# A four-layer graph network on one core: seven products of 384 columns in layer 3, the last two groups kept side by side, due times set anew

## The chip, the core and the metric

The kernel runs on one core of a Trainium2 chip. The core has TensorE (PE, matrix products, whose weight loads stand in the profile as PEld), VectorE (DVE), ScalarE (ACT), GpSimd (POOL) and DMA queues. The metric is the device time of one execution in microseconds; times given for the kernel are medians of several runs. Everything is computed in float32.

## The reference

There are 128 graphs of 64 nodes with 256 features. Four layers follow each other, each of the form "normalize over the features, take the positive part, apply the layer, add the result to x":

```
h = max(layernorm(x), 0);  x = x + layer_i(h)

layers 0, 1: masked attention, 8 heads of 32 features, softmax over the 64 nodes of a graph
layer 2:     five times: m = h @ weight[l]; agg = A^T m
             gi = agg @ w_ih^T + b_ih;  gh = h @ w_hh^T + b_hh
             r, z = sigmoid(i_r + h_r), sigmoid(i_z + h_z);  n = tanh(i_n + r * h_n)
             h = (1 - z) * n + z * h
layer 3:     norm = (sum |adj| + 1e-6) ** -0.5
             f = (h @ theta) * norm;  f_hom = (adj @ f) * norm
             f_het = h @ W_h;  gate = sigmoid(h @ W_t + b_t)
             elu(gate * f_hom + (1 - gate) * f_het)
```

The change concerns the three products of layer 3 (theta, W_t, W_h, each 256 by 256) and the order in which the work of all layers is issued.

## The kernel before

**Tiling.** Two graphs make a pair of 128 tokens, four pairs a group of 512 tokens, and a half is two pairs. There are 16 groups. Nothing is exchanged between groups, so the work of several stands side by side.

**Stages of a group.** `front` (line 909) does the attention of layers 0 and 1, one half after the other (`attend`, line 496), and prepares what the adjacency gives: A, norm and the transposed adjacency adjT. `entry` (957) normalizes x into h, transposed, for layer 2. `gru` (702) is a generator: each `next` adds one of the five steps of layer 2. `back` (966) takes the two halves of layer 3 through `back_half` (971): h is transposed back (hx, 978) and added to x, x is normalized into hT (through L452 and L457), and then each pair has its products: f (998), two matmuls of 256 columns, and gate (1004), two of 512, with W_t and W_h beside each other in w_th. DVE scales f by norm (1001), adds b_t (1007), ACT takes the tanh (1009) and copies het (1010). The product with adjT is hom (1011). Elementwise work follows to the store (1029).

**Layer 2 as it is already.** The GRU's products are taken as seven block products in place of eight (Winograd's form of Strassen's scheme): a product of two 2 x 2 block matrices needs seven block products if sums and differences of blocks are formed first. `combine` (648) forms those of the weights on GpSimd, once; `pre` (707) on GpSimd and `less` (795) on DVE form those of the data. The products accumulate in PSUM banks, which ACT copies out (`saved`, 806) and DVE adds (`summed`, 812) between products. In the profile all these matmuls stand at line 744. The weights of layer 2 are multiplied with w_ih before (`fuse_weights`, 662; products at 681), kept in DRAM, and loaded again for each step (`gv`).

**What sets the order.** Each operation is recorded in a `Plan` with an engine, an estimated cost, and what it reads and writes. `Plan.strand(base, span)` gives the recorded operations keys from base to base + span, along their TensorE work; a key is a due time in units of a group. `Plan.run` (165) first moves keys back so that an operation is due before what needs it, then plays the engines forward: it takes, over all engines, the operation that can start first, and among those that can start at about the same time the one of smallest key, as long as its key lies within AHEAD of the earliest open one. The order so found is written out, and each engine works through its own part in order. An operation that needs a buffer which isn't free can't be taken; the buffers are `Slots`, and those of the tags g, ht, agg, Ta, Th, gv, qT, kexp and v are given out in the order in which they were recorded. PSUM has four banks of tag "a" (attention, transposes, agg, layer 3) and four of tag "g" (the GRU's gates and the fusion of weights).

**Due times before (lines 1035 to 1062).** The first fronts have -1 to 0. The fusion of step l has -1 + 0.15 l, span 0.15. Front g + 1 has g, span 0.8; entry g - 0.1; step l of group g has g + 0.4 l - 0.2, span 0.4; back g + 2.2, span 0.9.

Of the kernel before, what the change touches and what calls it, by code (L numbers as in the profile page):

```python
# [10 lines left out]
AF = mybir.ActivationFunctionType  # L11
# [33 lines left out]


SWITCH, BESIDE, ALONE = 200, 0.3, 0.1
AHEAD = 1.2


def mm(n, count=1):
# [183 lines left out]
def gnn_stack_kernel(ctx: ExitStack, tc: tile.TileContext, a: dict, out: bass.AP):  # L235
# [18 lines left out]
    def new(tag, shape, n, name=None):  # L254
        if tag not in tags:
            home = psum if tag in ("a", "g") else dram if tag == "gates" else work
            tags[tag] = Slots(home, tag, n, tag in ("g", "ht", "agg", "Ta", "Th", "gv", "qT", "kexp", "v"))
        return Val(tags[tag], name or tag, shape)
# [17 lines left out]
    def sca(cost, fn, reads, writes, early=0.0):  # L276
        plan.add("ACT", cost, fn, reads, writes, early=early)
# [4 lines left out]
    def dma(kb, fn, reads, writes, n=1):  # L282
        plan.add("SP", max(450 * n, 60 + kb * 5), fn, reads, writes)
# [37 lines left out]
    def load_w(name, cols):  # L321
        t = new(f"w_{name}", [P, 2, cols], 1)
        dma(cols, lambda: nc.sync.dma_start(t.tile, a[name].rearrange("(c p) o -> p c o", p=P)), [], [t])
        return t
# [88 lines left out]
    with plan.strand(-0.3, 0.1):  # L413

        b_rz = new("b_rz", [P, 4], 1)
        vec(160, lambda: nc.vector.tensor_add(b_rz.tile, cols[:, 4:8], cols[:, 10:14]), [cols], [b_rz])
        vec(160, lambda: nc.vector.tensor_scalar(b_rz.tile, b_rz.tile, 0.5, None, op0=ALU.mult),
            [b_rz], [b_rz])


        b_n = new("b_n", [P, 2], 1)
        vec(160, lambda: nc.vector.tensor_sub(b_n.tile, cols[:, 8:10], cols[:, 14:16]), [cols], [b_n])

        theta = load_w("L3_gnn_theta", D)
        w_th = new("w_th", [P, 2, 2 * D], 1)
        for i, name in enumerate(("L3_gnn_W_t", "L3_gnn_W_h")):
            dma(256, lambda i=i, name=name: nc.sync.dma_start(
                w_th[:, :, i * D : (i + 1) * D], a[name].rearrange("(c p) o -> p c o", p=P)),
                [], [(w_th, i)])
        b_t = load_row("L3_gnn_b_t")  # L430
        blk = filled("adjblk", [P, PAIRS, P], 0.0)

# [212 lines left out]
        pe(470, weigh, reads, po, holds=[oT], small=True)  # L645
        finish()

    def combine(part, at):

        def one(dst, x, y, op):  # L650
            pool(1050, lambda: nc.gpsimd.tensor_tensor(at(dst), at(x), at(y), op=op), [part], [part])

        one(4, 1, 3, ALU.add)
        one(5, 4, 0, ALU.subtract)
        one(6, 2, 5, ALU.subtract)
        one(1, 0, 1, ALU.subtract)

# [2 lines left out]
    def fuse_weights(l):  # L662
# [7 lines left out]
                    nc.tensor.transpose(ps[:, ec * D + kc * P : ec * D + (kc + 1) * P],  # L670
                                        gw[l][:, kc, ec * P : (ec + 1) * P], ident.tile)

        wT = new("cp", [P, 2, D], 4, f"wT_{l}")
        pe(437, turn, [gw[l], ident], [ps], holds=[wT, gv])
        sca(act(512), lambda ps=ps, wT=wT: nc.scalar.activation(
            wT.tile, ps.tile.rearrange("p (c e) -> p c e", c=2), AF.Copy), [ps], [wT])
# [25 lines left out]
    def gru(h, ht, A, name):  # L702
# [19 lines left out]
        for l in range(LAYERS):  # L722
# [81 lines left out]
            less(3, lambda lo=lo: lo(1), lambda Ta=Ta: Ta[:, 1, :], [agg, (Ta, 1)])  # L804

            def saved(bk, n):
                t = new("cp", [P, 2, HALF], 4, f"{n}_{nm}")
                sca(act(512), lambda: nc.scalar.activation(
                    t.tile, bk.tile.rearrange("p (g t) -> p g t", g=2), AF.Copy), [bk], [t])
                return t  # L810
# [98 lines left out]
    def front(g):  # L909
# [38 lines left out]
        def turn():  # L948
# [1 line left out]
                nc.tensor.transpose(ps[:, p * P : (p + 1) * P], blk[:, p, :], ident.tile)  # L950

        pe(437, turn, [blk, ident], [ps], holds=[adjT])
        sca(act(512), lambda: nc.scalar.activation(
            adjT.tile, ps.tile.rearrange("p (t n) -> p t n", t=PAIRS), AF.Copy), [ps], [adjT])
        held[g] = xt, A, adjT, norm

    def entry(g, xt):

        h = new("h", [P, 2, TOK], 3, f"h_{g}")
        ht = new("ht", [P, PAIRS, D], 2, f"ht0_{g}")  # L960
        for half in range(2):
            norm_relu_t(xt, half, h, lambda half=half: h[:, :, half * HALF : (half + 1) * HALF],
                        [(h, (0, half)), (h, (1, half))], f"{g}_2_{half}", ht)
        return h, ht

    def back(g, xt, h, adjT, norm):

        for half in (1, 0):
            back_half(g, xt, h, adjT, norm, half)

    def back_half(g, xt, h, adjT, norm, half):
        ps = bank(f"hx_{g}_{half}")
# [9 lines left out]
        for i in range(2):  # L982
# [3 lines left out]
                xt[:, p, :], ps[:, i * D : (i + 1) * D], cols[:, 18 + t : 19 + t], xt[:, p, :],  # L986
                op0=ALU.mult, op1=ALU.add), [ps, cols, (xt, p)], [(xt, p)])
        hT = normed(xt, half, f"{g}_3_{half}")
        for p in range(2 * half, 2 * half + 2):
            nm = f"{g}_{p}"  # L990
            s = slice((p % 2) * P, (p % 2 + 1) * P)
            f = new("f", [P, D], 1, f"f_{nm}")
            gt = new("gt", [P, D], 2, f"gt_{nm}")
            het = new("het", [P, D], 2, f"het_{nm}")
            o = new("o", [P, D], 2, f"o3_{nm}")
            pf, pg, ph = bank(f"f_{nm}"), bank(f"gate_{nm}"), bank(f"hom_{nm}")
            for kc in range(2):
                pe(mm(256), lambda kc=kc, s=s, pf=pf: nc.tensor.matmul(  # L998
                    pf[:, :D], hT[:, kc, s], theta[:, kc, :], start=kc == 0, stop=kc == 1),
                    [hT, theta], [pf], holds=[f])  # L1000
            vec(dve(256, 1), lambda p=p, f=f, pf=pf: nc.vector.tensor_scalar(
                f.tile, pf[:, :D], norm[:, p : p + 1], None, op0=ALU.mult), [pf, norm], [f])
            for kc in range(2):
                pe(mm(512), lambda kc=kc, s=s, pg=pg: nc.tensor.matmul(  # L1004
                    pg.tile, hT[:, kc, s], w_th[:, kc, :], start=kc == 0, stop=kc == 1),
                    [hT, w_th], [pg], holds=[gt, het])
            vec(dve(256), lambda gt=gt, pg=pg: nc.vector.tensor_tensor(gt.tile, pg[:, :D], b_t.tile, op=ALU.add),
                [pg, b_t], [gt])
            sca(act(256, 0.3), lambda gt=gt: nc.scalar.activation(gt.tile, gt.tile, AF.Tanh, scale=0.5), [gt], [gt])
            sca(act(256), lambda het=het, pg=pg: nc.scalar.activation(het.tile, pg[:, D:], AF.Copy), [pg], [het])  # L1010
            pe(mm(256), lambda p=p, f=f, ph=ph: nc.tensor.matmul(
                ph[:, :D], adjT[:, p, :], f.tile, start=True, stop=True), [adjT, f], [ph], holds=[o])

            vec(dve(256, 1), lambda p=p, o=o, ph=ph, het=het: nc.vector.scalar_tensor_tensor(
                o.tile, ph[:, :D], norm[:, p : p + 1], het.tile, op0=ALU.mult, op1=ALU.subtract),
                [ph, norm, het], [o])
            vec2(dve(256), lambda o=o, gt=gt: nc.vector.scalar_tensor_tensor(
                o.tile, gt.tile, 1.0, o.tile, op0=ALU.add, op1=ALU.mult), [gt, o], [o])
            vec2(dve(256), lambda o=o, het=het: nc.vector.scalar_tensor_tensor(
                o.tile, o.tile, 0.5, het.tile, op0=ALU.mult, op1=ALU.add), [o, het], [o])  # L1020

            vec2(210, lambda o=o, gt=gt: nc.vector.tensor_scalar(gt.tile, o.tile, 0.0, None, op0=ALU.min),
                [o], [gt])
            sca(act(256, 0.3), lambda gt=gt: nc.scalar.activation(gt.tile, gt.tile, AF.Exp), [gt], [gt])
            vec2(dve(256), lambda o=o, gt=gt: nc.vector.scalar_tensor_tensor(
                o.tile, o.tile, 0.0, gt.tile, op0=ALU.max, op1=ALU.add), [o, gt], [o])
            vec2(dve(256), lambda p=p, o=o: nc.vector.scalar_tensor_tensor(
                xt[:, p, :], o.tile, -1.0, xt[:, p, :], op0=ALU.add, op1=ALU.add), [o, (xt, p)], [(xt, p)])
        dma(256, lambda: nc.sync.dma_start(
# [4 lines left out]

    held, chains = {}, {}
    parts = {g: front(g) for g in range(n_groups)}
    with plan.strand(-1.0):
        for g in (0, 0, 1, 0, 1, 0):
            next(parts[g])
        for _ in parts[0]:  # L1040
            pass
    for l in range(LAYERS):
        with plan.strand(-1.0 + 0.15 * l, 0.15):
            fuse_weights(l)
    with plan.strand(-0.2, 0.1):
        combine(w_hh, lambda b: w_hh[:, :, b, :])
    for at, g, l in sorted((g + 0.4 * l, g, l) for g in range(n_groups) for l in range(LAYERS)):
        if l == 0:
            xt, A, adjT, norm = held[g]
            with plan.strand(g - 0.1, 0.1):  # L1050
                h, ht = entry(g, xt)
            held[g] = xt, h, adjT, norm
            chains[g] = gru(h, ht, A, str(g))
            if g + 1 < n_groups:
                with plan.strand(g, 0.8):
                    for _ in parts[g + 1]:
                        pass
        with plan.strand(at - 0.2, 0.4):
            next(chains[g])
        if l + 1 == LAYERS:  # L1060
            with plan.strand(g + 2.2, 0.9):
                back(g, *held.pop(g))
    plan.run()

# [32 lines left out]
```

## Time and profile before

| what | value |
|---|---|
| median of 3 runs | 2589.91 us (2588.77 to 2590.13) |
| span of the profiled run | 2587.4 us |
| busy: PE, PEld | 2550.2, 2149.8 us |
| busy: DVE, ACT, POOL | 1863.6, 1357.7, 844.8 us |
| matmuls at line 744 (GRU), passes of 256 columns | 6720 |
| gate at line 1004, passes of 512 columns | 256 |
| f at line 998, passes of 256 columns | 256 |
| f scaled, L1001 | 64 times, 479 ns |
| gate + b_t, L1007 | 64 times, 419 ns |
| het copied, L1010 | 64 times, 383 ns |

A float32 matmul of the code stands in the trace as two passes with a weight load each. A pass's own duration overlaps its neighbours' (a pass of 256 columns is shown with 380 ns), so passes are best counted from start to start. "Idle before" is the time that an engine waited, with the operation that released it.

### The profile page before, as it was taken

The page shows a single profiled execution, that of the slowest core. Times are in us where ns is not written, and L with a number is a line of the kernel's source. Part 1 is how long each engine was busy: PE and PEld are TensorE (multiplying, and loading weights), DVE is VectorE, ACT ScalarE, POOL GpSimd, SP SyncE. Part 2 cuts the span into 40 slices and gives each one's busy share as a digit, 9 for nine tenths or more (in the row PEclk, how much of TensorE's full clock was granted, in tenths as well). Part 3 has the DMA queues.
Part 4 walks back from the last instruction along what each step waited for, and adds up shares of the span by engine and source line. Part 5 has one row for each costly group of instructions (what it writes and reads, how often), then busy time and mean ns, then how long its engine had stood idle before and what let it go on. Part 6 is the DMA issues. An engine that isn't in the chain of part 4 may idle for free.

```text
span 2587.4 us, 54651 instructions
## 1 busy us (share of the span) xinstructions
PE 2550.2 (99%) x22505; PEld 2149.8 (83%) x22505; DVE 1863.6 (72%) x3986; ACT 1357.7 (52%) x2536; POOL 844.8 (33%) x881
## 2 busy tenths in 40 slices
PE   8999999999999999999999999999999999999997
PEld 6788888888888888888888888888888888888875
DVE  5676767777776777767777677776777777777666
ACT  4455555454555546545565555645446554555443
POOL 5433333333333333333333333333332323323221
PEclk9999999999999999999999999999999999999998
DMA  5311111111111111121111111111120110211110
GB/s 171 113 52 46 42 69 44 60 44 48 60 48 61 43 44 60 48 77 44 48 60 48 56 44 64 44 48 56 48 78 23 65 60 26 77 44 52 65 52 17
DMA packets 44204, 145.55 MB, mean 56 GB/s; under 512 B 11106, under 2 KB 32820, under 8 KB 33076
## 3 DMA queue, kind: packets, MB, share of 16 engines
q1 hardware_dynamic: 43840, 142.03, 15.4%
q8 instruction: 177, 2.90, 0.4%
q14 instruction: 71, 0.58, 0.1%
q10 hardware_dynamic: 116, 0.04, 0.0%
HBM read 126.79 MB, written 15.27 MB: 55 GB/s over the span
## 4 chain that ended last, share of the span: by engine, by line
PE 96%; DVE 2%; ACT 1%; issue 0%; DMA 0%; POOL 0%; ACTq 0%; DVEq 0%
PE gb L744 21%; PE gc L744 16%; PE nb L744 11%; PE nc L744 8%; PE q L507 4%; PE y L634 4%; PE v L567 4%; PE gate L1004 4%; PE k L507 4%; PE agg L784 3%; PE s L547 3%; PE hT L452 2%; PE aT L602 2%; PE lnT L452 2%; PE f L998 2%; PE o L621 2%
## 5 line engine op out<-in xcount | busy, mean ns | idle before, releaser
L853 POOL TENSOR_TENSOR sn<-h,sn 128x512 f32<-128x512 f32 x160 | 204.8, 1280 | 745.2 <-ACT sn L851 745.0
L596 POOL TENSOR_TENSOR e<-e,ssum 128x512 f32<-128x512 f32 x128 | 131.7, 1047 | 378.6 <-DVE ssum L595 295.2
L744 PE MATMUL gb<-Th,w_hh 128*128 128x256 f32 x960 | 248.6, 381 | 0.0
L744 PE MATMUL gb<-Ta,gv 128*128 128x256 f32 x960 | 248.5, 381 | 0.0
L744 PEld LDWEIGHTS gb<-Th,w_hh 128*128 128x128 f32 x960 | 178.6, 190 | 30.6 <-issue 4.6
L744 PEld LDWEIGHTS gb<-Ta,gv 128*128 128x128 f32 x960 | 179.3, 190 | 26.2 <-issue 3.3
L713 POOL TENSOR_TENSOR Th<-h 128x256 f32<-128x256 f32 x160 | 115.9, 744 | 255.4 <-PE nb L744 186.9
L851 ACT ACTIVATE sn<-sn,b_n 128x512 f32<-128x512 f32 x160 | 115.6, 723 | 148.8 <-DVE sn L849 146.0
L438 POOL TENSOR_TENSOR rstd<-pw,mhalf 128x2 f32<-128x2 f32 x128 | 113.4, 886 | 178.3 <-DVE pw L437 156.3
L744 PE MATMUL gc<-h,w_hh 128*128 128x256 f32 x640 | 166.1, 382 | 0.0
L847 DVE SCALAR_TENSOR_TENSOR sn<-sg,sn 128x512 f32<-128x512 f32 x160 | 117.6, 735 | 65.9 <-ACT sn L901 62.5
L744 PE MATMUL gc<-agg,gv 128*128 128x256 f32 x640 | 164.3, 379 | 0.0
L855 DVE SCALAR_TENSOR_TENSOR sn<-sg,sn 128x512 f32<-128x512 f32 x160 | 121.4, 758 | 44.7 <-POOL sn L853 44.4
L836 ACT ACTIVATE sg<-sg,b_rz 128x512 f32<-128x512 f32 x160 | 108.9, 714 | 65.5 <-DVE sg L816 65.1
L744 PE MATMUL nb<-Th,w_hh 128*128 128x256 f32 x480 | 143.0, 380 | 0.0
L744 PE MATMUL nb<-Ta,gv 128*128 128x256 f32 x480 | 142.8, 379 | 0.0
L744 PEld LDWEIGHTS gc<-agg,gv 128*128 128x128 f32 x640 | 121.5, 190 | 16.5
L567 PE MATMUL v<-w_L_gnn_Wv,hT 128*128 128x256 f32 x512 | 133.9, 380 | 0.9 <-DVE qT L519 0.8
L744 PEld LDWEIGHTS gc<-h,w_hh 128*128 128x128 f32 x640 | 117.6, 190 | 20.7 <-issue 3.6
L1004 PE MATMUL gate<-w_th,hT 128*128 128x512 f32 x256 | 132.8, 602 | 0.0
L713 POOL TENSOR_TENSOR Th<-h,Th 128x256 f32<-128x256 f32 x160 | 128.1, 801 | 13.7 <-DVE h L857 7.9
L507 PE MATMUL q<-hT,w_L_gnn_Wq 128*128 128x256 f32 x512 | 128.2, 386 | 3.5 <-DVE e L583 1.9
(147 smaller groups left out, 6335.8 us busy)
## 6 DMA issues: line engine op xcount, KB each, us to landing
gv<-gates SPq DMA_DIRECT2D x80, 1344.0 KB, 5.7
x<-in_x_dram SPq DMA_DIRECT2D x32, 256.0 KB, 3.0
out_dram<-x SPq DMA_DIRECT2D x32, 256.0 KB, 2.2
gates<-gv SPq DMA_DIRECT2D x5, 1344.0 KB, 6.4
adjq<-in_adj_dram SPq DMA_DIRECT2D x8, 256.0 KB, 4.8
gw<-in_L_gnn_weight_dram SPq DMA_DIRECT2D x5, 256.0 KB, 6.5
w_ih<-in_L_gnn_w_ih_dram SPq DMA_DIRECT2D x2, 384.0 KB, 5.7
w_hh<-in_L_gnn_w_hh_dram SPq DMA_DIRECT2D x2, 384.0 KB
```

Of the source, the lines that this page charges most:

```text
L438: pool(1050, lambda: nc.gpsimd.tensor_tensor(dst.tile, s.tile, mhalf[:, :n], op=ALU.pow), [s, mhalf], [dst])
L507: pe(mm(256), lambda c=c, kc=kc: nc.tensor.matmul(ps[:, c * HALF : (c + 1) * HALF], wt[:, kc, c * P : (c + 1) * P], hT[:, kc, :], start=kc ...
L567: pe(mm(256), lambda gp=gp, kc=kc: nc.tensor.matmul(pv[:, gp * D : (gp + 1) * D], hT[:, kc, gp * P : (gp + 1) * P], w["v"][:, kc, :], star ...
L596: pool(1090, lambda e8=e8, z=z: nc.gpsimd.tensor_tensor(e8(), e8(), z[:, :, None].to_broadcast(shape), op=ALU.mult), [e, z], [e])
L713: pool(790, lambda: nc.gpsimd.tensor_tensor(T[:, i, :], x(), y(), op=ALU.subtract), reads, [(T, i)])
L744: nc.tensor.matmul(bank_[:, col * HALF : (col + 1) * HALF], at(g, n), rhs(), start=first and j == 0, stop=True, skip_group_check=True)
L836: sca(act(TOK, 1), lambda k=k, col=col: nc.scalar.activation(g_v[:, :, k, :], g_v[:, :, k, :], AF.Tanh, bias=b_rz[:, col : col + 1], scale ...
L847: vec2(dve(TOK), lambda: nc.vector.scalar_tensor_tensor(a_(), r(), 1.0, a_(), op0=ALU.add, op1=ALU.mult), [*ts[0], n_v], [n_v])
L851: sca(act(TOK, 1.3), lambda: nc.scalar.activation(a_(), a_(), AF.Tanh, bias=b_n[:, oc : oc + 1]), [n_v, b_n], [n_v])
L853: pool(TOK * 1.85 + 320, lambda: nc.gpsimd.tensor_tensor(b_(), hh(), a_(), op=ALU.subtract), [*hp, n_v], [n_v])
L855: vec2(dve(TOK, 1), lambda: nc.vector.scalar_tensor_tensor(b_(), z(), 1.0, b_(), op0=ALU.add, op1=ALU.mult), [*ts[1], n_v], [n_v])
L1004: pe(mm(512), lambda kc=kc, s=s, pg=pg: nc.tensor.matmul(pg.tile, hT[:, kc, s], w_th[:, kc, :], start=kc == 0, stop=kc == 1), [hT, w_th], ...
```

## The change

**Layer 3 in seven products.** theta, W_t and W_h are loaded as 128 x 128 blocks into one tile w3, and `combine` forms their sums and differences once. A half's 256 tokens by 256 features are a 2 x 2 block matrix, and so are the weights, each block being 128 by 3 x 128 columns (theta, W_t and W_h beside each other). `seven_products` takes seven matmuls of 384 columns per half in place of the eight of that size that the plain form amounts to; DVE forms four differences of hT, and ACT and DVE bring the results through two PSUM banks into F, which holds f, gate and het of a pair. The last group keeps the plain products (`plain_products`). The scaling of f by norm is moved into adjT: four ACT instructions scale its columns where one copied it.

**The last two groups side by side.** The last group's GRU is due 0.35 of a group earlier (LOCK), its steps 0.2 later (STEP_LAST), and the backs of the last two groups have due times of their own, so that work of both stands beside each other up to the end.

**Due times anew.** Fronts are due from g - 1.1 over a span of 1.0, backs from g + 1.9 over 0.5, the fusion of step l from -1 + 0.45 l over 0.45, AHEAD is 1.5. There are five buffers cp in place of four and four of h in place of three.

The core of the diff:

```
-AHEAD = 1.2
+AHEAD = 1.5
+FRONT = -0.1
+FRONT_LAST = -0.05
+FRONT_SPAN = 1.0
+BACK = -0.1
+BACK_LAST = 0.5
+BACK_SPAN = 0.5
+STEP = -0.2
+STEP_LAST = 0.2
+STEP_SPAN = 0.4
+LOCK = 0.35
+BACK_END = 0.25
+ENTRY = -0.15
+FIRST = -1.0
+FIRST_SPAN = 0.9
+FUSE = -1.0
+FUSE_SPAN = 0.45
...
-        theta = load_w("L3_gnn_theta", D)
-        w_th = new("w_th", [P, 2, 2 * D], 1)
+        w3 = new("w3", [P, 3, 8, P], 1)
...
-        sca(act(512), lambda: nc.scalar.activation(
-            adjT.tile, ps.tile.rearrange("p (t n) -> p t n", t=PAIRS), AF.Copy), [ps], [adjT])
+        for p in range(PAIRS):
+            sca(act(P, 1), lambda p=p: nc.scalar.activation(
+                adjT[:, p, :], ps[:, p * P : (p + 1) * P], AF.Identity, scale=norm[:, p : p + 1]),
+                [ps, norm], [(adjT, p)])
...
+    def seven_products(hT, F, name):
+        T = new("hTT", [P, 4, P], 1, f"hTT_{name}")
...
+            vec2(dve(128), lambda n=n, x=x, y=y: nc.vector.tensor_tensor(T[:, n, :], x(), y(), op=ALU.subtract),
+                 [hT, *reads], [(T, n)])
+        pb, pc = bank(f"l3b_{name}"), bank(f"l3c_{name}")
...
+        product(1, pb, True)
+        product(2, pc, True)
+        total(pc, keep(pb, "l1"), 0, 0)
+        product(5, pc, True)
+        p5 = keep(pc, "l5")
+        product(6, pb)
+        u = keep(pb, "lu")
+        product(3, pc)
+        total(pc, u, 0, 1)
+        product(7, pb)
+        total(pb, p5, 1, 1)
+        product(4, pb)
+        sca(act(384), lambda: nc.scalar.activation(F[0][:, :, P:], part(pb), AF.Copy), [pb], [(F[0], 1)])
...
+        F = [new("F", [P, 3, D], 3, f"F_{g}_{2 * half + i}") for i in range(2)]
+        if g + 1 == n_groups:
+            plain_products(hT, F, f"{g}_{half}")
+        else:
+            seven_products(hT, F, f"{g}_{half}")
...
+    begin = {g: g - (LOCK if g + 1 == n_groups else 0.0) for g in range(n_groups)}
+    events = sorted([(begin[g] + 0.4 * l, g, l) for g in range(n_groups) for l in range(LAYERS)] +
+                    [(begin[g] - 1.001, g, -1) for g in range(1, n_groups)])
...
-        with plan.strand(at - 0.2, 0.4):
+        with plan.strand(at + STEP + (STEP_LAST if last else 0), STEP_SPAN):
             next(chains[g])
         if l + 1 == LAYERS:
-            with plan.strand(g + 2.2, 0.9):
+            with plan.strand(begin[g] + 2 + BACK + (BACK_LAST if g + 2 == n_groups else BACK_END if last else 0), BACK_SPAN):
                 back(g, *held.pop(g))
```

## The prediction

> **What bounds the kernel now.** I read the page's busy shares first, then the table of stretches, and TensorE's timeline at the end.
>
> ```profile
> span 2587.4 us, 54651 instructions
> PE 2550.2 (99%) x22505; PEld 2149.8 (83%) x22505; DVE 1863.6 (72%) x3986; ACT 1357.7 (52%) x2536; POOL 844.8 (33%) x881
> ...
> PE 96%; DVE 2%; ACT 1%; issue 0%; DMA 0%; POOL 0%; ACTq 0%; DVEq 0%
> ```
>
> TensorE is busy 99% of the span and makes up 96% of the chain that ended last. A busy share can hide slack inside matmuls, so I looked at the stretches (length, then busy time of PE, PEld, DVE, ACT, POOL, then clock):
>
> ```profile
> 20.00:40.00 20.00, 19.65 (x115) 14.01 (x114) 12.51 (x29) 11.21 (x24) 11.16 (x11) 1.00 0.35 122
> 40.00:60.00 20.00, 19.06 (x236) 13.89 (x240) 14.64 (x28) 9.57 (x21) 14.95 (x16) 1.00 0.35 116
> ...
> 80.00:100.00 20.00, 18.36 (x173) 14.04 (x172) 13.66 (x33) 11.38 (x22) 11.00 (x11) 1.00 0.57 202
> 100.00:150.00 50.00, 46.11 (x550) 39.00 (x549) 34.61 (x82) 24.70 (x44) 16.33 (x18) 1.00 0.12 38
> ...
> 200.00:300.00 100.00, 98.67 (x897) 84.79 (x897) 68.70 (x131) 54.30 (x100) 35.63 (x36) 1.00 0.15 56
> 300.00:2400.00 2100.00, 2100.00 (x18824) 1783.05 (x18823) 1539.63 (x3288) 1125.79 (x2103) 682.64 (x703) 1.00 0.15 52
> ...
> 2450.00:2500.00 50.00, 47.44 (x283) 39.79 (x282) 35.30 (x76) 23.19 (x44) 12.40 (x14) 1.00 0.21 76
> 2500.00:2520.00 20.00, 18.81 (x146) 15.92 (x146) 12.47 (x32) 8.49 (x16) 3.30 (x4) 1.00 0.04 14
> 2520.00:2540.00 20.00, 19.12 (x146) 14.96 (x145) 12.09 (x27) 9.31 (x19) 4.57 (x5) 1.00 0.05 15
> 2540.00:2560.00 20.00, 14.93 (x62) 11.24 (x60) 15.80 (x37) 7.95 (x17) 2.55 (x2) 0.88 0.00 0
> 2560.00:2580.00 20.00, 16.54 (x46) 9.38 (x46) 11.86 (x33) 4.49 (x12) 1.39 (x2) 0.78 0.07 26
> ```
>
> The kernel has three regimes. In the 2100 us of the middle TensorE never waits, so only fewer passes can shorten it. Between 20 and 300 us it is idle 0.35 + 0.94 + 1.64 + 3.89 + 1.33 = 8.2 us, with the skipped stretches adding 0.1. From 2450 to 2580 us it is idle 2.56 + 1.19 + 0.88 + 5.07 + 3.46 = 13.2 us, at a lowered clock at the end. Outside these, the first 7.6 us wait for loads and the last 7 us are elementwise work and the store.
>
> The timeline of TensorE (start, length, operation, idle time before it) gives the prices and the tail:
>
> ```profile
> 2523.52 1.02 PE L1004 MATMUL gate<-w_th,hT 128*128 128x512 f32 x2
> 2524.38 1.03 PE L998 MATMUL f<-w_L_gnn_theta,hT 128*128 128x256 f32 x4
> 2525.24 1.02 PE L1004 MATMUL gate<-w_th,hT 128*128 128x512 f32 x2
> ...
> 2555.98 1.76 PE L978 MATMUL hx<-ident,h 128*128 128x128 f32 x7 [2.38 <-DVE h L857]
> 2561.63 1.13 PE L452 MATMUL lnT<-ident,xn 128*128 128x128 f32 x4 [3.89 <-DVE xn L478]
> 2563.45 2.07 PE L998 MATMUL f<-w_L_gnn_theta,hT 128*128 128x256 f32 x4 [0.69 <-ACT hT L457]
> 2565.31 3.57 PE L1004 MATMUL gate<-w_th,hT 128*128 128x512 f32 x4
> ```
>
> From start to next start, two passes of 512 columns take 0.86 us (0.430 each) and four of 256 take 0.86 us (0.216 each). Each matmul of the code is two passes. In the tail the chain of group 15 alone (h, transpose, layer norm) leaves TensorE nothing to do, and the passes after it run at half rate.
>
> **What the Trainium skill says.** "Perfetto Trace Analysis", Identifying the Most-Contended Engine: matmul busy time is no good measure of how near TensorE is to its limit. That is why I rest on start intervals; they show 0.216 us again and again, so the pipe is full here. "TensorE: Matmul & The Clock Gate", Part 1: a gap is N/2.4 plus 2.5 ns when warm, and an idle window of about 3.4 us halves the clock. The fixed part being small agrees (0.430 is nearly twice 0.216); the slope does not, since these float32 passes cost 0.84 ns a column at clock 1.00, and the measurement decides. The halving agrees: after idle times of 2.38 and 3.89 us the four passes of f take 1.86 us to the next start in place of 0.86. "VectorE: DVE Perf Modes", on the errata: an fp32 tensor_tensor costs (N+151)/0.96 ns. That gives 424 for 256 columns; the trace has 443 (Ta from agg and Ta) and 417 (L1017).
>
> **The change, part by part.**
>
> *Seven products.* A half of a group (two pairs) now takes 8 passes of 512 and 8 of 256: 8 x 0.430 + 8 x 0.216 = 5.17 us. Seven products of 384 columns are 14 passes. No pass of 384 is in the trace; the mean of 0.216 and 0.430 is 0.323. So 14 x 0.323 = 4.52 us, 0.65 less. The moving operand now comes in three runs of 128 columns with gaps. From below it costs nothing more; from above I allow a fixed 0.0025 per run (the page's fixed part), 14 x 2 x 0.0025 = 0.07 us per half, an estimate. I take nothing. The last group keeps the plain products, so 30 halves save 30 x 0.65 = 19.4 us (17.3 at the other end). Nearly all lie in the middle, where passes are the time.
>
> *What the seven products cost the other engines.* Per half DVE loses two f scalings (479 ns, L1001) and two gate additions from PSUM (419, L1007), 1.80 us. It gains four subtractions of 128 columns at 0.29 (the errata formula; 443 at 256 bounds it from above), three sums of 384 from PSUM at 0.55 (between 419 at 256 and 687 at 512), and two gate additions in SBUF at 0.43: 3.67 us. That is +1.9 us, 56 us over 30 halves, so DVE goes to about 1920 us, 75%. ACT loses two copies of 383 and gains four of 384 columns at 0.49 (between 383 and 596): +1.2 us, 36 us in all. The scaling of adjT by norm, four ACT instructions of 128 columns in place of one of 596 ns, is about 4 x 0.37 (slope of L843 at 501 to L836 at 714, carried down; 0.3 is the lower bound): +0.9 us a group, 14 us. ACT then has about 1408 us, 55%. Four more GpSimd combinations at 1.2 us (the w_hh row) come once. All this I cost at nothing: it lies beside 2100 us of unbroken TensorE work, and each engine keeps a quarter of its time or more free.
>
> *The added waits.* Products 5, 3, 6, 7 and 4 go into a bank that ACT or DVE must have read first. Behind each wait stands all of TensorE's in-order queue. A wait from product to copy to sum to product is about 0.5 + 0.55 + latencies of some 0.4, about 1.5 us; about four such waits are 6 us per half if nothing were put between, 180 us over 30 halves. The other end is zero, because Plan.run places GRU passes between them exactly as it does for the same pattern of L744, which shows 0.0 us idle in 6720 passes' groups but for 1.9 us. I take zero. The two held banks leave two of the four "a" banks to the scores and to agg, which take two at once.
>
> *Weight fusion later (FUSE).* The fused weights' products are 25 us of passes (80 of L681, half of 512: 40 x 0.43 + 40 x 0.216 = 26) that now end near 90 us, just before the idle times of 90 to 130 us begin. Spread out, they can fill those. All must have taken their "g" banks before group 0's first GRU product, since that queue is in order, so they can't drift far. Of 8.2 us I take 5 as won.
>
> *Last groups side by side (LOCK, STEP_LAST, BACK_LAST, BACK_END).* Group 15's GRU starts 0.35 of a group earlier and its steps 0.2 later: 0.15 of 157 us, 23 us, nearer to group 14's. The back of group 14, layer 3 of the model, is due later, so that it is kept for the end. Of 13.2 us idle plus 2.7 us from half-rate passes (f: 1.86 less 0.86; four of gate: 3.41 less 1.72), some stays: group 15's own last chain still has to run, and only some 13 us of group 14's passes can stand beside it. I take 6.
>
> *FRONT, BACK, AHEAD, ENTRY, more cp and h buffers:* in the middle there is no idle to win; I cost them at nothing.
>
> Sum: 2589.9 - 19.4 - 5 - 6 = 2559.5 us.
>
> **Rivals.** (a) The due times earn nothing, the products earn all: 2589.9 - 19.4 = 2570.5. For it: the idle times at both ends are chains of one group, and work given to one gap is taken from another. Against: half of the start's idle lies after the fusion has run out. (b) Both ends are filled: 2589.9 - 19.4 - 8 - 13 = 2549. For it: the fill exists. Against: the last layer norm and products have no partner. (c) Slower: the new waits show. If a fifth of the 180 us came through, 36 - 19.4 + 2589.9 = 2606; with the ends' gains 2596. For it: four "a" banks, DVE at 75% and in order, three buffers for F. Against: the same pattern stalls nowhere now.
>
> **How the numbers follow.** Forecast 0.57, (a) 0.19, (b) 0.12, (c) 0.12. Predicted is 2559.5. The lower end is at (b), 2549; the upper takes in (a) with the 384-column bound and a few us of middle waits, 2577. Faster by over 0.2% (under 2584.7) covers the first three, 0.88 less some slips, so 0.87; slower is most of (c), 0.09; 0.04 between.
>
> **What will show it.** 210 matmuls, 420 passes, of 384 columns at 0.323 us from start to start; a middle still without TensorE idle and a group period of 156.7 - 1.3 = 155.4 us; fewer than 4 us idle from 20 to 300; six fewer from 2450 on; DVE near 1920. I am wrong if a pass of 384 takes over 0.34, if waits of the new products on ACT or DVE appear in the middle, or if group 15's tail still stands alone.

## The result, and the profile after

The changed kernel takes **2576.55 us** (2576.26 to 2577.2) against 2590.02 (2588.77 to 2590.33) for the kernel before on the same chip: a ratio of 0.9949 [0.9932, 0.9966], 13.5 us less. The forecast was 30.5 us less. More than half of the expected gain did not arrive, and the question of the experiments is where it went.

The page's head for the changed kernel:

```profile
span 2574.5 us, 54704 instructions
PE 2537.9 (99%) x22445; PEld 2134.7 (83%) x22445; DVE 1885.6 (73%) x4136; ACT 1390.1 (54%) x2644; POOL 858.3 (33%) x885
```

Nothing here tells what went wrong: TensorE is still busy 99% of the span. The stretches say more (length, then busy time of PE, PEld, DVE, ACT and POOL, then the clock). First two of the kernel before, cut at the same places; its middle is in the prediction:

```profile
20.00:300.00 280.00, 271.78 (x2614) 224.49 (x2614) 194.82 (x404) 146.22 (x271) 118.15 (x122) 1.00 0.21 77
...
2400.00:2600.00 200.00, 167.51 (x1035) 133.87 (x1033) 122.23 (x268) 78.47 (x152) 39.48 (x43) 0.95 0.12 43
```

and the changed kernel:

```profile
20.00:300.00 280.00, 274.59 (x2630) 227.21 (x2628) 196.37 (x408) 152.40 (x288) 124.17 (x129) 1.00 0.22 79
300.00:2400.00 2100.00, 2096.05 (x18741) 1775.56 (x18740) 1560.66 (x3443) 1151.14 (x2193) 692.86 (x705) 1.00 0.15 53
2400.00:2600.00 200.00, 157.13 (x1044) 124.18 (x1042) 121.68 (x259) 79.94 (x154) 36.69 (x37) 0.97 0.11 38
```

- **Start.** Between 20 and 300 us the idle time falls from 8.2 to 5.4 us, not to below 4. The first 20 us have 0.8 us less work in them (10.1 us busy against 11.0), which is hardly more than this figure varies by itself: it is 10.4 in `before_no_ln` below, which has the order of the kernel before. The start is worth 2.0 us by this profile, up to 2.8 without that 0.8.
- **Middle.** 2100 us that were without a gap now have 3.95 us of idle time: small, but new.
- **End.** The last stretch runs to the end of the span, 187.4 us before and 174.5 after. Idle are 187.4 - 167.5 = 19.9 us before and 174.5 - 157.1 = 17.4 us after.

The new products cost what was forecast. TensorE's timeline (start, length, operation):

```profile
2509.99 0.81 PE L1032 MATMUL l3b<-w,hT 128*128 128x384 f32 x2
2510.63 0.81 PE L1032 MATMUL l3c<-w,hT 128*128 128x384 f32 x2
```

Two passes of 384 columns take 0.64 us to the next start. Over all passes of this size with nothing odd behind them the mean is 0.3227 us; by the same count 256 columns take 0.2159 and 512 take 0.4293. The group of L1032 holds 180 + 120 + 60 + 60 = 420 of them.

Whether the middle became shorter is best read from one and the same block of work two groups later. agg is such a block, and its starts lie one period of two groups apart. Before:

```profile
1656.38 1.16 PE L784 MATMUL agg<-A,ht 64*64 64x64 f32 x64
...
1969.72 1.16 PE L784 MATMUL agg<-A,ht 64*64 64x64 f32 x64
```

After, over four periods:

```profile
692.25 1.16 PE L807 MATMUL agg<-A,ht 64*64 64x64 f32 x64
...
1941.69 1.16 PE L807 MATMUL agg<-A,ht 64*64 64x64 f32 x64
```

Before, two groups take 313.3 us; after, (1941.69 - 692.25) / 4 = 312.4. Four halves in seven products should have taken off 4 x 0.644 = 2.6 us; 1.0 is there. **So most of the missing gain is in the middle, where the prediction saw nothing to lose.** The idle time there is only 3.95 us; the rest is passes that stand less well beside each other, and no busy share shows that.

The tail still ends in the chain of one group:

```profile
2550.62 0.78 PE L475 MATMUL lnT<-ident,xn 128*128 128x128 f32 x4 [3.16 <-DVE xn L501]
2552.08 2.07 PE L1003 MATMUL f<-w,hT 128*128 128x256 f32 x4 [0.69 <-ACT hT L480]
2553.95 2.59 PE L1007 MATMUL gate<-w,hT 128*128 128x512 f32 x4
2556.38 1.03 PE L1003 MATMUL f<-w,hT 128*128 128x256 f32 x4
```

The same wait for xn stands before the last layer norm, 3.16 us in place of 3.89. After it f takes 1.87 us to the next start in place of 0.86, and gate 2.43 in place of 1.72: 1.7 us of half-rate passes, where there were 2.7.

### The profile page after: what moved, and what is told of

It is laid out like the page before. It is cut to its first block, busy times and chain, and to the rows that moved or that the text cites. A ratio compares the mean times of both kernels' runs of the same rounds, so it can differ in the third digit from the quotient of the medians.

```text
span 2574.5 us, 54704 instructions
## 1 busy us (share of the span) xinstructions
PE 2537.9 (99%) x22445; PEld 2134.7 (83%) x22445; DVE 1885.6 (73%) x4136; ACT 1390.1 (54%) x2644; POOL 858.3 (33%) x885
## 4 chain that ended last, share of the span: by engine, by line
PE 95%; DVE 2%; ACT 1%; issue 0%; DMA 0%; POOL 0%; ACTq 0%; DVEq 0%; POOLq 0%
PE gb L767 21%; PE gc L767 17%; PE nb L767 11%; PE nc L767 8%; PE y L657 4%; PE q L530 4%; PE k L530 4%; PE v L590 4%; PE agg L807 3%; PE l3b L1032 3%; PE s L570 3%; PE hT L475 2%; PE lnT L475 2%; PE aT L625 2%; PE l3c L1032 2%; PE o L644 2%
## 5 line engine op out<-in xcount | busy, mean ns | idle before, releaser
L876 POOL TENSOR_TENSOR sn<-h,sn 128x512 f32<-128x512 f32 x160 | 214.3, 1339 | 686.3 <-ACT sn L874 685.1
L619 POOL TENSOR_TENSOR e<-e,ssum 128x512 f32<-128x512 f32 x128 | 140.1, 1106 | 353.7 <-DVE ssum L618 285.7
L839 DVE TENSOR_TENSOR sg<-gc,ug 128x512 f32<-128x512 f32 x80 | 55.2, 690 | 165.9 <-PE gc L767 163.7
L878 DVE SCALAR_TENSOR_TENSOR sn<-sg,sn 128x512 f32<-128x512 f32 x160 | 124.0, 775 | 61.8 <-POOL sn L876 61.5
L859 ACT ACTIVATE sg<-sg,b_rz 128x512 f32<-128x512 f32 x160 | 108.0, 715 | 99.0 <-DVE sg L839 98.3
L461 POOL TENSOR_TENSOR rstd<-pw,mhalf 128x2 f32<-128x2 f32 x128 | 99.6, 787 | 169.3 <-DVE pw L460 163.5
L596 POOL TENSOR_TENSOR x<-x,r_L_gnn_bo 128x512 f32<-128x512 f32 x64 | 110.0, 1719 | 87.7 <-DVE xn L501 78.4
L530 PE MATMUL k<-hT,w_L_gnn_Wk 128*128 128x256 f32 x512 | 130.6, 380 | 0.0
```

The costliest lines, as they stand in the source:

```text
L530: pe(mm(256), lambda c=c, kc=kc: nc.tensor.matmul(ps[:, c * HALF : (c + 1) * HALF], wt[:, kc, c * P : (c + 1) * P], hT[:, kc, :], start=kc ...
L596: pool(1250, lambda: nc.gpsimd.tensor_tensor(xt[:, pp : pp + 2, :], xt[:, pp : pp + 2, :], bo[:, None, :].to_broadcast([P, 2, D]), op=ALU. ...
L619: pool(1090, lambda e8=e8, z=z: nc.gpsimd.tensor_tensor(e8(), e8(), z[:, :, None].to_broadcast(shape), op=ALU.mult), [e, z], [e])
L859: sca(act(TOK, 1), lambda k=k, col=col: nc.scalar.activation(g_v[:, :, k, :], g_v[:, :, k, :], AF.Tanh, bias=b_rz[:, col : col + 1], scale ...
L876: pool(TOK * 1.85 + 320, lambda: nc.gpsimd.tensor_tensor(b_(), hh(), a_(), op=ALU.subtract), [*hp, n_v], [n_v])
L878: vec2(dve(TOK, 1), lambda: nc.vector.scalar_tensor_tensor(b_(), z(), 1.0, b_(), op0=ALU.add, op1=ALU.mult), [*ts[1], n_v], [n_v])
```

## Experiments

Each expectation below says what its theories are. The edits are to the changed kernel unless another is named; constants that change are written together on one line, though each has a line of its own in the kernel. Every run is set against the kernel before, timed beside it. That kernel's median is between 2589.59 and 2590.64 us in these comparisons, so differences between runs of different comparisons are good to about 1 us.

### The parts by themselves: products alone, due times alone

`products_alone` keeps the seven products and sets every due time back (the five cp and four h buffers stay):

```
-AHEAD, FRONT, FRONT_LAST, FRONT_SPAN = 1.5, -0.1, -0.05, 1.0
+AHEAD, FRONT, FRONT_LAST, FRONT_SPAN = 1.2, 0.0, 0.0, 0.8
-BACK, BACK_LAST, BACK_SPAN, BACK_END = -0.1, 0.5, 0.5, 0.25
+BACK, BACK_LAST, BACK_SPAN, BACK_END = 0.2, 0.0, 0.9, 0.0
-STEP_LAST, LOCK, ENTRY, FIRST_SPAN, FUSE_SPAN = 0.2, 0.35, -0.15, 0.9, 0.45
+STEP_LAST, LOCK, ENTRY, FIRST_SPAN, FUSE_SPAN = 0.0, 0.0, -0.1, 1.0, 0.15
```

> The seven products with the due times, AHEAD and the last group's place of the kernel before (five cp and four h buffers stay). Theory A, that the products save their 19.4 us and the loss in the middle comes from the order that the new due times give: 2590 - 19 = 2571, give or take 3, with next to no idle time of TensorE between 300 and 2400 us. Theory B, that the seven products bring their waits with them wherever they are placed: about 10 us of the 19.4 lost in the middle here too, 2580 or more.

Measured: **2813.01 us** against 2590.64, ratio 1.0862 [1.0847, 1.0877]. The sevenfold products, put into the old order, cost 222 us. No number expected was near. TensorE's longest waits (total, times, longest) and a piece of its timeline:

```profile
PE aT L625 <- POOL e L619: 63.2, 16, 4.8
PE hT L475 <- DVE h L880: 44.5, 20, 3.3
PE s L570 <- DVE x L1075: 24.6, 13, 2.4
```

```profile
1011.60 0.81 PE L1032 MATMUL l3b<-w,hTT 128*128 128x384 f32 x2
...
1022.01 1.98 PE L570 MATMUL s<-kexp,qT 64*64 64x128 f32 x30 [1.84 <-DVE x L1075]
1024.14 3.78 PE L657 MATMUL y<-w_L_gnn_Wo,oT 128*128 128x256 f32 x8 [0.15 <-DVE oT L652]
1032.72 2.12 PE L625 MATMUL aT<-ident,e 128*128 128x128 f32 x8 [4.80 <-POOL e L619]
```

None of these waits names the new products. The first is a link of attention's own chain (softmax e, then its transpose aT), the second one of the GRU's. The third is a wait for a bank: s doesn't read x, but the operation x at L1075 is what empties the bank of hx. The line of the timeline to see is the first: it is the last product of a half. Only after it, and after the copy that empties its bank, do the scores s start, and from 1014 to 1040 us attention's chain runs with next to nothing beside it. Eight passes of y are shown with 3.78 us here, at half rate; the same eight at 1038.62 us with 1.89. What held attention up until then is in the code: `attend` records the last weighting of one half and the scores of the next as **one operation, `both`**, which needs four "a" banks at once. There are four in all. As long as a half of layer 3 holds two of them, from its first product to its last copy, `both` can't start, and then everything it feeds comes late and in a row. From the trace, a half holds its banks 48 or 21 us here, 69 us a group; in the changed kernel it is 28 or 14, 42 a group. That `both` is the cause is an argument so far; `products_split` below tests it.

`times_alone` does the opposite, all groups with plain products under the new due times:

```
-        if g + 1 == n_groups:
+        if True:
```

> All due times and buffers of the kernel after, but every group takes the plain products of layer 3 (as only the last one does after). Theory A, that the new order itself costs the middle some 8 us and wins some 4 at the ends: 2590 or a few us more. Theory B, that the new order is good and the seven products cost the middle: 2586, the ends' win alone, with no idle time of TensorE between 300 and 2400 us.

Measured: **2592.56 us** against 2590.64, ratio 1.0009 [1.0003, 1.0016]. The new order by itself makes the kernel slower, although it shortens both ends. (This kernel also keeps the moved scaling by norm, the tile F and the added buffers, so the figure is for all of these together.) Its middle and its period:

```profile
300.00:2400.00 2100.00, 2096.56 (x18724) 1774.69 (x18723) 1536.75 (x3294) 1132.94 (x2128) 673.07 (x700) 1.00 0.15 52
```

```profile
1636.60 1.16 PE L807 MATMUL agg<-A,ht 64*64 64x64 f32 x64
...
1951.06 1.16 PE L807 MATMUL agg<-A,ht 64*64 64x64 f32 x64
```

314.46 us in place of 313.34. Over the 6.7 periods in the middle that is 7.5 us. Counted without the period, pass by pass at the prices above, the 2100 us of the middle hold 7.3 us more than before that are no work: 3.4 us of idle time, and 3.9 us in passes further apart. It agrees with the whole: 7.5 less the 5.5 that the ends win in the changed kernel makes 2.0, and 1.9 was measured. Against this kernel the seven products of the changed one are worth 2592.56 - 2576.55 = 16.0 us; the next experiment accounts for what is missing to 19.3.

### A table load in a chain: no_ln

ACT loads a table before the logarithm of attention's mask and another before the next sigmoid or tanh. In this stretch of the changed kernel (all engines, start, length, operation, idle time before it) one of them shows:

```profile
1299.62 1.28 ACT L859 ACT_TABLE_LOAD   x1
...
1300.92 1.33 ACT L859 ACTIVATE sg<-sg,b_rz 128x512 f32<-128x512 f32 x2
...
1301.67 0.69 DVE L870 SCALAR_TENSOR_TENSOR sn<-sg,sn 128x512 f32<-128x512 f32 x1 [1.23 <-ACT sg L859]
...
1302.28 0.55 DVE L1044 TENSOR_TENSOR F<-l3c,lu 128x384 f32<-128x384 f32 x1
...
1302.89 1.10 PE L570 MATMUL s<-kexp,qT 64*64 64x128 f32 x30 [0.47 <-DVE F L1044]
```

The load holds up sg by 1.28 us, sg holds up sn, and F, the sum that empties bank l3c, queues behind sn on DVE. The scores wait for F, that is, for the bank. The Trainium skill, "ScalarE: Activation LUTs", What ACT_TABLE_LOAD costs, gives 1283 ns for the load, which agrees (1283 ns mean in this trace), and about 1380 ns of draining on top, which does not: sg starts 0.02 us after the load ends. To price it, the logarithm becomes a line through its two values:

```
-NEG = -9000000000000000.0
+NEG = -9000000000000000.0; LN_SPAN = math.log(1 + 1e-6) - math.log(1e-6)
...
-            lambda: nc.scalar.activation(l.tile, t.tile, AF.Ln, bias=eps6.tile), [t, eps6], [l])
+            lambda: nc.scalar.activation(l.tile, t.tile, AF.Identity, bias=eps6.tile, scale=LN_SPAN), [t, eps6], [l])
...
-        eps6 = filled("eps6", [P, 1], 1e-6)
+        eps6 = filled("eps6", [P, 1], math.log(1e-6))
```

> The kernel after, with log(adj + 1e-6) taken as a line through its two values (adj is 0 or 1) by an Identity of the same size, so that ACT never changes its function table; the order of all instructions is the same. If the scores wait every second group (0.73 us longer, 5 times between 300 and 2400 us) because a table load of 1.28 us holds ACT before the sigmoid at L859, and DVE's sum behind it: those waits go and the time falls by 3 to 5 us, to about 2572. If the sums are late because the planner prices DVE too low or the banks are held too long: waits and time stay, 2576.

Measured: **2572.62 us** against 2590.64, ratio 0.9931 [0.9917, 0.9944]: 3.9 us under the changed kernel, with the period at 311.4 us. The five waits of the scores for F between 300 and 2400 us, 2.3 us together, are gone. The control `before_no_ln`, the same edit in the kernel before:

> Control for no_ln: the kernel before with the same line in place of the logarithm (adj is 0 or 1), so no change of ACT's function table; the order of instructions is the same. TensorE waits nowhere between 300 and 2400 us before, so the 16 table loads of 1.28 us lie in ACT's idle time and taking them away wins nothing there: within 1.5 us of 2590. If table loads cost by themselves, wherever they stand, as much as in the kernel after: 2586.

Measured: **2588.82 us** against 2590.15, ratio 0.9996 [0.9988, 1.0004]. The interval takes in 1, and TensorE is busy for all 2100.00 us from 300 to 2400 us with the loads and without them. What differs is where the second load stands. Among the groups of each kernel (count, then total us, mean ns and idle time before) it is, for the kernel before, the changed kernel and `close` below:

```profile
L851 ACT ACT_TABLE_LOAD x6 | 7.7, 1283 | 0.1
...
L859 ACT ACT_TABLE_LOAD x6 | 7.7, 1283 | 0.1
...
L1094 ACT ACT_TABLE_LOAD x6 | 7.7, 1283 | 0.1
```

L851 is the GRU's tanh, L859 its sigmoid, L1094 the tanh of layer 3's gate. So the load is not dear by itself; the changed kernel has put it ahead of a chain that ends in a bank.

### Side by side taken back: no_lock

```
-FRONT_LAST, BACK_LAST, STEP_LAST, LOCK, BACK_END = -0.05, 0.5, 0.2, 0.35, 0.25
+FRONT_LAST, BACK_LAST, STEP_LAST, LOCK, BACK_END = 0.0, 0.0, 0.0, 0.0, 0.0
```

> The kernel after without the special treatment of the last two groups (LOCK, FRONT_LAST, STEP_LAST, BACK_LAST, BACK_END all 0). If side by side earns the 3 to 4 us by which the tail's idle time and half-rate passes fell: 2580. If the tail's gain comes from elsewhere: within 1 us of 2576.5.

Measured: **2589.66 us** against 2590.64, ratio 0.9997 [0.9989, 1.0005]. Its last stretch:

```profile
2400.00:2600.00 200.00, 161.94 (x1059) 129.06 (x1058) 119.78 (x260) 81.96 (x154) 37.78 (x41) 0.94 0.12 43
```

188.8 - 161.9 = 26.9 us idle, 9.5 more than in the changed kernel, and a lower clock on top. Neither expected time was near. Within the new due times the edit is worth 13 us, much more than the 3.5 by which the tail is shorter than before: without it the new due times make the tail worse than it was (26.9 us idle against 19.9). My reading, not tested further, is that they bring the backs early, so that nothing is left for the tail, and that LOCK with its companions puts something back.

### Four banks at once: products_split and its control

`products_split` is `products_alone` with the one operation made two, each in need of two banks:

```
-            pe(1440, both, [*reads, qT, k_exp], [*po_last, *pss], holds=[oT_last, *es], small=True)
+            pe(470, weigh_last, reads, po_last, holds=[oT_last], small=True)
...
+            pe(870, scores, [qT, k_exp], pss, holds=es, small=True)
```

> The seven products with the due times of before, as in products_alone (2813 us), with one more edit: the operation that joins one half's weighted sums with the next half's scores, and needs all four 'a' banks of PSUM at once, is two operations of two banks each. Theory A, that attention stands still while the seven products hold two of the four banks: most of the 222 us go, about 2600. Rival, that the F buffers or the late backs hold everything up: the time stays above 2750.

Measured: **2603.66 us** against 2590.10, ratio 1.0053 [1.0039, 1.0066]. Of the 222 us, 209 are gone. The control, the same split in the kernel before:

> Control for products_split: the kernel before with the same joined operation taken apart. By every theory its plain products hold no two banks for long, so it costs a few us for switching between small and large matmuls, 0.2 us for each of 48 more blocks: 2590 to 2602.

Measured: **2594.66 us** against 2590.10, ratio 1.0018 [1.0011, 1.0024]: the split costs 4.6 us where banks are not short, so it is no gain by itself. (It has 13 more blocks of small matmuls, not the 48 expected, and 3.3 us of idle time before 600 us.) **That `both` needs its four banks together is the cause of 209 of the 222 us.** The remaining 9 us between the two kernels show that the products don't pay in the old order even then: the middle of `products_split` keeps 16 us of idle time.

```profile
300.00:2400.00 2100.00, 2083.84 (x18641) 1755.12 (x18639) 1586.28 (x3404) 1142.21 (x2180) 720.15 (x700) 1.00 0.15 52
```

### Which due time decides: back_old, nudge, fuse_old

`back_old` sets back only the backs:

```
-BACK, BACK_SPAN = -0.1, 0.5
+BACK, BACK_SPAN = 0.2, 0.9
```

> The kernel after with the due times of the backs alone set as before (from g + 2.2 over a span of 0.9 in place of g + 1.9 over 0.5). If the due times of the backs are what keeps the seven products' two banks from stopping attention: as bad as products_alone, 2750 to 2820, with the two banks held for some 70 us a group in place of 42. If other due times matter more: under 2650.

Measured: **2788.38 us** against 2590.10, ratio 1.0766 [1.0751, 1.078]. One pair of numbers brings back nearly the whole loss; with a span of 0.9 a half is seen to hold its banks for up to 102 us. So the new due times of the backs are no tuning of a tail: as long as `both` is one operation, they are what makes the seven products possible. Whether these due times, and not the others, also bring the new order's loss in the middle was not tested.

`nudge` has the backs 0.02 of a group later than the changed kernel:

```
-BACK = -0.1
+BACK = -0.08
```

> The kernel after with BACK at -0.08 in place of -0.1: each back due 0.02 of a group, 3 us, later. If the order is one lucky fit, found among many, between the seven products' two banks and the attention's operation on four: a clear loss, 2590 to 2615. If any back due near the end of its GRU does as well: within 3 us of 2576.5.

Measured: **2594.48 us** against 2590.15, ratio 1.0019 [1.0012, 1.0025]. Some 3 us of due time cost 18 us. The middle has 8.9 us of idle time in place of 3.95, and the period is 314.6 us in place of 312.3:

```profile
300.00:2400.00 2100.00, 2091.10 (x18685) 1767.56 (x18684) 1529.22 (x3429) 1156.79 (x2184) 721.75 (x700) 1.00 0.15 52
```

A longer hold of the two banks is not what went wrong here: a half holds them 8 us or 20 to 26, 32 a group, which is less than the 42 of the changed kernel. What comes back in every group is three short waits (0.17, 0.40 and 0.21 us), none of them of the new products. To this side, at least, the changed kernel stands at an edge.

`fuse_old` sets back the fusion of weights:

```
-FIRST_SPAN, FUSE_SPAN = 0.9, 0.45
+FIRST_SPAN, FUSE_SPAN = 1.0, 0.15
```

> The kernel after with FUSE_SPAN 0.15 and FIRST_SPAN 1.0 as before: the weight fusion early and close together. The idle time of TensorE from 20 to 300 us fell by 2.8 us from before to after; if the later fusion earns it, 2579 to 2582 here. If it came from elsewhere: within 1 us of 2576.5.

Measured: **2579.99 us** (2576.77 to 2580.07) against 2590.10, ratio 0.9955 [0.9942, 0.9969]. The later fusion earns about 3.4 us by the medians, while the lowest of its five runs reaches the changed kernel's time; the idle time of 20 to 300 us is 6.4 in place of 5.4. The profiled run is one of the long ones, and not all of its excess is the start's. The wait for xn before the last layer norm ends 2.4 us later than in the changed kernel; behind it gate takes 3.41 us to the next start in place of 2.43, more half-rate passes in the tail:

```profile
2556.60 3.62 PE L1007 MATMUL gate<-w,hT 128*128 128x512 f32 x4
2560.01 1.16 PE L1003 MATMUL f<-w,hT 128*128 128x256 f32 x4
```

So the start's gain is some 2.4 us in this run, and the rest belongs to the tail.

### Shorter holds: close_no_ln, close

If long holds are the trouble, the products of a half should stand close together. `close_no_ln` makes them due at nearly one time, moves three due times a little to suit, and keeps the line in place of the logarithm, to see the middle without table loads:

```
-BACK, STEP_LAST, ENTRY = -0.1, 0.2, -0.15
+BACK, STEP_LAST, ENTRY = -0.05, 0.15, -0.05
+EARLY = 0.97
...
-        pb, pc = bank(f"l3b_{name}"), bank(f"l3c_{name}")
+        pb, pc = bank(f"l3b_{name}"), bank(f"l3c_{name}"); at0 = [plan.at]
...
-                [w3, *reads], [bk], holds=F)
+                [w3, *reads], [bk], early=EARLY * (plan.at - at0[0]), holds=F)
```

> no_ln (2572.6 us) with the seven products of a half due nearly at one time, so that they stand close together, and BACK -0.05, STEP_LAST 0.15, ENTRY -0.05 to fit. If holding the two banks (28 and 14 us for the halves of a group) costs the middle its remaining loss: shorter holds and a period of two groups under 311 us, 2566 to 2570. If that loss is the new order's switching and short waits, whatever the hold: 2571 to 2575.

Measured: **2569.01 us** against 2590.15, ratio 0.9917 [0.9904, 0.9931]. `close` is the same with the logarithm in its place, the whole computation:

> close_no_ln (2569.0 us) with the logarithm put back, so that ACT changes its function table twice every second group; it computes all of the reference. If a table load costs only where something is queued close behind it: between 2569 and 2573, and TensorE's idle time between 300 and 2400 us tells which (0.3 us in close_no_ln). If each reload costs what it did in the kernel after: 2573, with a repeated wait of about 0.7 us every 311 us.

Measured: **2568.25 us** (2567.96 to 2569.49) against 2589.59, ratio 0.9917 [0.9903, 0.9931]. It is faster than both kernels. Its middle and its period:

```profile
300.00:2400.00 2100.00, 2099.75 (x18834) 1781.22 (x18833) 1593.40 (x3460) 1158.62 (x2203) 718.17 (x706) 1.00 0.15 53
```

```profile
1656.05 1.16 PE L808 MATMUL agg<-A,ht 64*64 64x64 f32 x64
...
1967.35 1.16 PE L808 MATMUL agg<-A,ht 64*64 64x64 f32 x64
```

A half holds its banks 12 or 7 us, 19 a group. TensorE is idle 0.25 us in the middle, and the period is 311.3 us. The table loads are as many as before and cost nothing here: `close` and `close_no_ln` differ by less than their spread. The expected time came, but the reason given for it did not hold. The period was to fall under 311 us, and it is 311.3 against the 311.4 of `no_ln`: holds of less than half the length are worth 0.1 us per two groups. Of the 4 us between the spans of `no_ln` and `close_no_ln`, 1.1 are there by 600 us and some 2 arise from 2200 us on, where the last groups join. So the 8.3 us under the changed kernel are the order's as a whole (no waits behind a table load, and better ends), and not the shorter hold's.

## Why the prediction was wrong

The sum on record was 2589.9 - 19.4 - 5 - 6 = 2559.5. Term by term:

| term | predicted | measured | read from |
|---|---|---|---|
| seven products | -19.4 | -19.3 | 30 halves x (8 x 0.2159 + 8 x 0.4293 less 14 x 0.3227) |
| due times in the middle | 0 | +7.5 | period of the due times alone, 314.46 against 313.34, x 6.7 |
| waits behind a table load | 0 | +3.9 | changed kernel less the one without the logarithm |
| start | -5 | -2.0 | idle 8.2 to 5.4, first 20 us 0.8 more |
| last groups | -6 | -3.5 | idle 19.9 to 17.4, half-rate passes 2.7 to 1.7 |
| sum | -30.4 | -13.4 | measured as a whole: -13.5 |

The measured terms come from several runs and are good to half a us or so each; that their sum meets the whole so closely is in part luck.

**The step that failed** is "in the middle there is no idle to win; I cost them at nothing", said of FRONT, BACK, AHEAD and ENTRY. An engine without idle time has next to nothing to win by a new order, but it can lose: 1.1 us per two groups, 7.5 in all. I took a saturated engine for one whose work is a fixed sum of passes. It isn't. The middle of `times_alone` against that of the kernel before, from 300 to 2400 us, shows three kinds of loss:

- 3.4 us of idle time, where there was none.
- Single intervals between passes that are longer than their price with no wait shown, most of them by 0.10 us: 163 in place of 131, 16.4 us in place of 13.0. What stretches them I don't know.
- Blocks of small matmuls (64 rows): the last pass of 256 columns ahead of a block takes 0.309 us in place of 0.216, and the last matmul of the scores takes 0.199 us to a large pass but 0.089 to another block. So a block that stands alone costs some 0.2 us. There are 133 in place of 129, which makes 0.8 us.

**The second step** is "I take zero" for the added waits. The new products themselves hardly wait (all waits of L1032 and of scores for F are 4.4 us together, and one of L1032, 0.2 us, lies in the middle), as I argued from the GRU's pattern. But I looked for the wait at the products, and it falls on the scores. "The two held banks leave two of the four 'a' banks to the scores and to agg, which take two at once" is wrong for `both`, which takes four, as its line in `attend` says (po_last and pss, two banks each). Rival (c) named the four banks as its reason and gave them a fifth of 180 us. In the old order it is 222 us, more than that whole bound. The new due times for the backs, which I had priced at nothing, are what avoids this. A third wait was not thought of at all: the one behind a table load, 3.9 us. A hint was in the skill: "Perfetto Trace Analysis", Optimization Strategy, says that a gap that repeats on the engine that should be saturated can mean that there is not enough SBUF or PSUM for the next tile; the waits of `products_alone`, 63.2 us in 16 pieces on one line, are of this kind, with the bank some steps upstream of the line that is shown.

**Mis-sized** are start and tail. The start keeps 5.4 us of idle time where I left 3.2, and its first 20 us lose 0.8. In the tail I gave group 14's passes to group 15's last chain; they now stand beside it earlier, but the last wait for xn is as good as alone (3.16 us); of the signs of being wrong that I had named, this one came. By `no_lock` the term of -3.5 is a balance of two: side by side wins 13.1 us, and the new due times, priced at nothing, cost the tail the difference, some 9.6, of which 7.0 is idle time.

**Right** were the price of a pass of 384 columns (0.323 forecast and measured, so that the three runs of 128 columns add nothing to the mean of 256 and 512), and the reserve of the other engines: DVE has 1886 us in place of 1920, ACT 1390 in place of 1408. The single terms of DVE were close (sums of 384 columns 0.55 us as forecast, subtractions of 128 a mean of 0.33 to 0.39 in place of 0.29); other DVE work became some 40 us cheaper in all, which I have not traced and which makes the total better than its terms.

Rival (a), "the due times earn nothing", gave 2570.5 and was nearest, though for a different reason: they earn 5.5 us at the ends and lose more in the middle, but without them the products cost 222 us. **The parts can't be added**: products alone +222, due times alone +1.9, both -13.5.

What stays open: why the number of stretched intervals depends on the order (`close` has 148, and its period is still 0.5 us above the old one less the products, 310.8); which of the new due times brings the loss in the middle; and why the later fusion is worth 2.4 us at the start when its idle times show 1.

## What to carry to other kernels

Before you let one stage hold a buffer longer, list every operation that takes several of the same pool at one time: the one that needs all of them is shut out for the whole hold, and the waits then show up at its followers and not at the holder. On an engine that never idles a new order is not free; compare the distance between two recurrences of the same block, since busy shares will not tell. Where a change has parts that make each other possible, run each alone as well as both. And look at what a better time rests on: the shorter hold looked like the reason for the fastest kernel here, and the period shows that it was not.

## What the runs showed of the hardware that was not expected

- The 16 ACT table loads that come with the logarithm, 1.28 us each, cost 3.9 us of 2576.55 in one order, and nothing measurable in two others with the same number of loads.
- A float32 pass costs 0.216, 0.323 and 0.429 us for 256, 384 and 512 columns. The 512 columns cost the same in one run (before) and in two runs of 256 (`times_alone`); the 384 columns come in three runs of 128 and lie on the same line.
- A block of 64-row matmuls costs some 0.09 us ahead of it (0.309 us to its start in place of 0.216) and 0.11 behind it (0.199 in place of 0.089); where two blocks stand together this is saved once.
- TensorE's passes have intervals that are stretched by some 0.10 us with no wait in the profile: 131 of them in the 2100 us of the middle before, 163 in `times_alone`, which has the same passes.
